# Reordering the weighing and scoring of head pairs in a two-layer graph attention kernel

## The chip, the cores and the metric

The kernel runs on one core of a Trainium2 chip. The metric is the device time of one execution in microseconds (us), as the median of several runs. The engines are called as in the profile: PE is TensorE (matmuls), PEld its weight loads, DVE is VectorE, ACT is ScalarE, POOL is GpSimd, and SP is SyncE, which only issues DMAs here. ACTq and SPq are DMAs issued from the queues of ScalarE and SyncE.

## The reference

64 graphs of 256 nodes with 512 features pass through two attention layers. Each layer normalises, applies a ReLU, attends over the graph's edges and adds the result to its input:

```python
# layer 0: 4 heads of 64, no bias on q, k, v
h = jnp.maximum(_layernorm(x, axis=-1), 0.0)
q, k, v = split_heads(h @ Wq), split_heads(h @ Wk), split_heads(h @ Wv)
sim = jnp.einsum('bhid,bhjd->bhij', q, k) * 64 ** -0.5
attn = jax.nn.softmax(jnp.where(adj[:, None], sim, -jnp.finfo(sim.dtype).max), axis=-1)
out = jnp.einsum('bhij,bhjd->bhid', attn, v)            # heads joined again
x = x + out @ Wo + bo
# layer 1: 8 heads of 64; a second layernorm with gamma and beta after the ReLU,
# the mask is adj | eye, masked scores are -1e9
h = jnp.maximum(_layernorm(x, axis=-1), 0.0)
...
x = x + out @ w_out.T + b_out
```

All matrices are float32.

## The kernel before

**Steps and periods.** `fast_path` takes two graphs in a step, so there are 32 steps `s`. (`general_path` is there for inputs with extreme scores and is entered only when a flag says so.) Work of several steps overlaps: in one *period* the kernel finishes layer 1 of step `s`, finishes layer 0 of step `s+1` and starts layer 0 of step `s+2`. In the profile a period lasts about 96.8 us; one visit at AT_X starts at 1553.24 us and the next at 1650.0.

**The order written by hand.** Instructions of PE, DVE, ACT and POOL are issued in the order in which the program makes them. That order is a list: `at(period, place, fn, ...)` (L1126) notes a piece of work with a number, and at the end (L1366) all pieces are sorted by it and run. Pieces with the same number keep the order in which they were noted. A place is about one product set of 12 us per unit, but between pieces that are close together only the order counts: 0.00002 after something means "right behind it on every engine that both use". DMAs of SyncE are issued by the same functions.

**Dense products.** Projections and output products are done in seven block products instead of eight (`project_qk` L805, `project_v0_turned` L855, `project_v1` L890, `combine` L905), each into a PSUM bank, with sums of blocks taken by ACT, DVE and POOL (`evacuate` L746, `accumulate` L765, `act_sums0` and `act_sums1` L404 to L410). The fourth product of a set adds into the bank of the first, so the first must have been copied out by ACT (L751, L759 or L770) before. [...] four go round as `ps_sc` ("sc" in the profile), four as `ps_mm` ("mm").

**Visits.** Between the dense sets stand visits (`visit`, L1143), three to a period: at AT_X before `project_v1`, at AT_Q0 before layer 0's projections, and at AT_Z before layer 1's first. A visit at place `w` takes heads in pairs `pr`. It *weighs* the two pairs of a previous unit, that is, it multiplies the exponentials with the values (`weigh`, L1034, matmuls at L1041, form 128\*32), and copies the result out on ACT (`weigh_out`, L1056). It *scores* the two pairs of a new unit (`scores`, L957, matmuls at L970, form 64\*128), adds the mask on DVE (`mask_scores`, L993, four instructions for each pair), and takes exponentials on ACT (`exponentials`, L998, four for each pair). Below, W0 and W1 are the weighings of the two pairs, S0 and S1 the scorings. W0 uses one sc bank, W1 one mm bank; S0 uses four sc banks; S1 uses two mm banks for the first graph and two sc banks for the second. In the kernel before, PE does W0, S0, W1, S1. Later, POOL adds halves of the keys (`key_halves`, L1005), DVE transposes and sums them (`turn_keys` L1011, `key_quarters` L1018, then L1071 to L1083), and POOL scales the weighed values by the inverse sums (`normalise`, L1116).

**Work beside a visit that the change touches.**

- `turn_values` (L874, DVE, one transpose at L878) turns layer 0's values, made by `project_v0_turned`, into a tile `values` that uses the same memory (tag "turned") as layer 1's `h`. It stands in the visit at AT_Z, behind the masks of S0.
- `place_h` (L714, ACT at L725 for layer 1) places the transposed `h` in `hT`, in four pieces `c`. Pieces 0 and 1 stand before the visit at AT_Z, at AT_H1; pieces 2 and 3 behind W0's copy.
- `scale_row` (L604, ACT at L606) scales one of the four row tiles of `h`. All four stand in the visit at AT_Q0 between W0's copy and the exponentials of S0. `turn_blocks` (L695, DVE at L700) reads them later.
- `load_graph` (L498, DMA from ACT's queue at L502) loads a step's `x` again, one graph at a time, into a buffer that `store_graph` (L947) empties. Both loads stand at AT_X behind W1's copy; POOL's `first_bias` (L508) reads them.

Of the kernel before, what the change touches and what calls it, by code (L numbers as in the profile page):

```python
# [315 lines left out]
def fast_path(  # L316
# [24 lines left out]
    NSTEP = B // G  # L341
# [62 lines left out]
    def act_sums0(b, eng=nc.gpsimd):  # L404
        eng.tensor_tensor(b[:, 3], b[:, 5], b[:, 0], ALU.subtract)
# [8 lines left out]
    HC, HP0, HP1 = NC // 2, PR0 // 2, PR1 // 2  # L414
# [711 lines left out]
    def at(period, place, fn, *args):  # L1126
        events.append((period * (PERIOD if period >= 0 else FIRST) + place, len(events), fn, args))

    def at_dense(period, place, length, fn, *args):

        rest = []
        at(period, place, lambda: rest.append(fn(*args)))
        at(period, place + length - LAST, lambda: rest[0]())

    def at_set(period, place, order, fn, *args):
        for i, n in enumerate(order):
            at_dense(period, place + i / 7, 1 / 7, fn, *args, n)
# [5 lines left out]
    def visit(period, w, prev, cur):  # L1143

        w -= 0.0003
        s, lyr, prs = prev
        last = (s, lyr) == (NSTEP - 1, 1)
        if prs:
            if prs[0] == 0 and not last:
                at(period, w - 0.0002, place_values, s, lyr)  # L1150
            if (s, lyr) == (1, 0):
                turned = sums = 0, 0.88
            elif 0 <= period < NSTEP - 2:
                sums = turned = (
                    (period, AT_X + 1.45) if abs(w - AT_Q0) < 0.01 else
                    (period, AT_V0 + 0.5595) if abs(w - AT_Z) < 0.01 else (period - 1, AT_Z + 1.25)
                )
                if abs(w - AT_Z) < 0.01:
                    turned = period, AT_V0 + 0.41
            else:  # L1160
                turned = sums = period, w - 0.0001
            at(*turned, turn_sums, s, lyr, prs)
            at(*sums, key_sums, s, lyr, prs)
            at(period, w - 0.00008, inverse_in, s, lyr, prs)
            for i, pr in enumerate(prs):
                if not last:
                    at(period, w + 0.0002 * i, weigh_out, s, lyr, pr, i == 1)
                    at(period, w + (0.55 if len(prs) == 1 else (0.3, 0.75)[i]), normalise, s, lyr, pr)
        z, q = w > AT_Z - 0.01 and period < NSTEP - 2, abs(w - AT_Q0) < 0.01 and 0 <= period < NSTEP - 2
        for i, pr in enumerate(cur[2]):  # L1170
            unit = (*cur[:2], pr)
            one = cur[:2] == (0, 0)
            at(period, w + 0.0002 * i, scores, *unit, i == 1)
            at(period, w + 0.0002 * i, mask_scores, *unit, 0)
            at(period, w + 1 / 7 if one else w + 0.0002 * i, mask_scores, *unit, 1)
            both = len(cur[2]) == 2
            for g, place in enumerate((0.05, 0.22) if one else ((0.00015, 0.00016) if both else (0.02, 0.03), (0.15, 0.3))[i]):
                at(period, w + place, exponentials, *unit, g)
            for e, place in enumerate((0.23, 0.3) if one else ((0.1, 0.11), (0.495, 0.496) if z else (0.435, 0.436) if q else (0.35, 0.36))[i]):
                if unit == (1, 0, 1):  # L1180
                    at(0, 0.45 + place, key_halves, *unit, e)
                else:
                    at(period, w + place, key_halves, *unit, e)
            if cur[:2] == (1, 0):
                period, w, key = 0, 0.0, (*cur[:2], (0, 1), pr)
                turn, add = ((0.44, 0.441), (0.715, 0.87))[pr]
            else:
                turn, add = (
                    ((0.31, 0.311), (0.6583, 0.6585))[pr] if one else ((0.49, 0.491), (0.63, 0.92))[i] if z else
                    ((0.43, 0.431), (1.02, 1.021))[i] if q else ((0.29, 0.291), (0.715, 1.001 if w < AT_X else 0.87))[i]  # L1190
                )
                key = (*cur, i)
            at(period, w + turn, turn_keys, cur[0])
            at(period, w + add, key_quarters, *key)

    AT_X, AT_C0, AT_QK, AT_Q0, AT_V0, AT_H1, AT_Z = 2.0, 3.0, 3.5, 4.5, 5.5, 6.06, 6.2
    LAST_QK = 4.0
    none, L0, L1A, L1B = (NSTEP, 0, ()), (0, 1), (0, 2), (1, 3)
    for s in range(NSTEP - 1):
        visit(s, AT_X, (s + 1, 0, L0), (s, 1, L1A))  # L1200
        if s < NSTEP - 2:
            visit(s, AT_Q0, (s, 1, L1A), (s, 1, L1B))
            visit(s, AT_Z, (s, 1, L1B), (s + 2, 0, L0))

    p = NSTEP - 2
# [15 lines left out]
    for s in range(NSTEP):  # L1221

        p = s - 2
# [41 lines left out]
        if s < 2:  # L1265
            for t in range(NT):
                place = (FIRST_V0 + 0.14 * t - (0 if t else 0.0005), (4.31, 5.02, 5.16, 5.31)[t])[s]
                at_dense(p, place, 0.14, project_v0, s, t)
        else:
            for i, n in enumerate(SET):  # L1270
                at_dense(p, AT_V0 + 0.08 * i, 0.08, project_v0_turned, s, n)
            at(p, AT_Z - 0.0002, turn_values, s)
            at(p, 6.6, move_values, s, 0)
            at(p, 6.98, move_values, s, 1)
        p = s - 1
        if s == 0:
            p -= 2.23 / FIRST
        edge = 0 if s == 0 else 1 if s == NSTEP - 1 else 2
        if edge < 2:
            at(p, (0.0, 0.2)[edge], load_x, s)  # L1280
        else:
            at(p, AT_X + 0.005 if s > 1 else 1.2, load_graph, s, 1)
            at(p, AT_X + 0.0051 if s > 1 else 1.2, load_graph, s, 0)
        for k, t in enumerate(NORM1):
            at(p, (1.55, 1.5, (2.34, 2.5, 2.85, 2.86)[k])[edge], first_bias, s, t)
# [10 lines left out]
        for k in range(NT):  # L1296
            at(p, ((2.901, 3.041, 3.181, 3.321), (2.99919, 2.99933, 2.99947, 2.99961), (3.79, 3.8, 3.94, 3.95))[edge][k], norm1, s, k)
            at(
                p, ((3.042, 3.182, 3.322, 3.323), (2.99948, 3.2, 3.3, 3.45), (4.08, 4.22, 4.23, 4.37))[edge][k],
                norm1_rest, s, k,  # L1300
            )
            at(*((0, 3.6 + 0.001 * k), (p, 6.5 + 0.1 * k), (p, 5.6 + 0.01 * k))[edge], second_bias, s, k)
            place = ((3.6112, 3.6113, 3.7502, 3.7503)[k], 3.6 + 0.01 * k, AT_Q0 - 0.0002 + 0.00001 * k)[edge]
            at(p, place, scale_row, s, NORM1[k])
            if edge == 2:
                at(p, AT_Q0 + (0.15, 0.16, 0.29, 0.3)[k], turn_blocks, s, 1, NORM1[k])
# [2 lines left out]

        turn = (3.763, 3.9995, AT_H1)[edge]  # L1310
        for c in range(NC):
            at(
                p, turn + 0.00001 * c if edge < 2 or c < HC else AT_Z - 0.00029 + 0.00001 * c,
                transpose_h if edge < 2 else place_h, s, 1, c,
            )
        at(p, turn + (0.001, 0.0001, 0.155)[edge], lambda s=s: act_sums0(S[s]["hT"]))
        at(p, turn + (0.002, 0.0001, 0.156)[edge], lambda s=s: act_sums1(S[s]["hT"]))
        p = s
        if s < NSTEP - 1:
            at_set(p, 0.0, SET, project_qk, s, 1, 0)  # L1320
            at_set(p, 2.0, SET, project_v1, s)
            at_set(p, AT_QK if s < NSTEP - 2 else 3.0, SET, project_qk, s, 1, 1)
            p, place = (s + 1, 1.0) if s < NSTEP - 2 else (s, LAST_QK + 2)
            at(p, place - 0.24, lambda s=s: act_sums0(S[s]["oT1"]))
            at(p, place - 0.23, lambda s=s: act_sums1(S[s]["oT1"]))
            at_set(p, place, SETC, combine, s, 1)
            at(p, place + 6 / 7 + 0.001, store_graph, s, 1)
            at(p, place + (0.99975 if s < NSTEP - 2 else 0.9994), store_graph, s, 0)
        else:
            p = s - 1  # L1330
            at_set(p, LAST_QK, SET, project_qk, s, 1, 0)
            at_set(p, LAST_QK + 1, SET, project_qk, s, 1, 1)
            at_set(p, LAST_QK + 3, SET, project_v1, s)
            at(p, LAST_QK + 4.015, lambda s=s: act_sums0(S[s]["oT1"], nc.vector))
            at(p, LAST_QK + 4.035, lambda s=s: act_sums1(S[s]["oT1"], nc.vector))
            at_set(p, LAST_QK + 4.1, SETC, combine, s, 1)
            for n, (i, j) in enumerate(((0, 0), (0, 1), (1, 1), (1, 0))):
                at(p, LAST_QK + 4.1 + (3, 6, 5, 7)[n] / 7, store_block, s, i, j)
# [14 lines left out]
    for i in range(16):  # L1353

        place = (
            *(3.3 - 3.93 + (1 + k) / 7 - 0.0005 for k in range(7)), 0.5205,
            *(0.53 + 0.14 * (k + 1) - 0.0005 for k in range(4)), *(FIRST + (2 + k) / 7 - 0.0005 for k in range(4)),
        )[i]
# [61 lines left out]
```

## Time and profile before

| | us |
|---|---|
| median of 3 runs | 3144.71 |
| lowest and highest | 3144.18, 3145.71 |
| the profiled execution | 3143.63 |
| its span, first to last instruction | 3141.5 |
| granted TensorE clock | 1.0 of full speed |

The span is shorter than the time of the same execution by 2.1 us, which lie before the first and after the last instruction. The costliest groups on the engines that a visit uses, from part 5 of the profile's page (busy us, mean ns of one):

| line and engine | what | count | busy us | mean ns |
|---|---|---|---|---|
| L970 PE | scoring, sc banks | 2320 | 296.5 | 386 |
| L1041 PE | weighing, sc banks | 3152 | 190.8 | 382 |
| L993 DVE | mask, sc banks | 579 | 361.6 | 678 |
| L998 ACT | exponentials | 766 | 433.0 | 624 |
| L606 ACT | scale_row | 252 | 184.9 | 805 |
| L1005 POOL | key_halves | 383 | 479.3 | 1274 |

Matmuls are pipelined: one is listed with 380 ns although the next starts 216 ns after it. So times between starts say more than durations or busy time.

### The profile page before, as it was taken

The numbers are of one execution on the slowest core, as the hardware profiler recorded it, in microseconds if no ns is written. First come the engines' busy times: TensorE is split into PE (matmuls) and PEld (weight loads), VectorE is DVE, ScalarE is ACT, GpSimd is POOL, SyncE is SP. The second block draws the span as 40 slices with busy tenths as digits, with TensorE's granted clock in tenths as the row PEclk, the third lists the DMA queues.
The fourth block names the chain that finished last, engine by engine and source line by source line (L and its number), as shares of the span: only waits on it lengthen the run. The fifth ranks groups of instructions, "written<-read, shape, count | busy, mean of one in ns | idle before, by whom it ended". The sixth has DMA issues, their size and how long they took to land.

```text
span 3141.5 us, 55627 instructions
## 1 busy us (share of the span) xinstructions
PE 3125.5 (99%) x20362; PEld 2524.9 (80%) x20362; DVE 2462.6 (78%) x4371; ACT 1218.3 (39%) x2166; POOL 2244.6 (71%) x2128
## 2 busy tenths in 40 slices
PE   9999999999999999999999999999999999999999
PEld 7887888887888878788787888888787878878777
DVE  6877877878877778777787777877777877778766
ACT  4434343334334343433434333343434343343431
POOL 7877776776767767767777677776776766777753
PEclk9999999999999999999999999999999999999999
DMA  4233132232222332223313233222232222331211
GB/s 140 62 96 92 52 93 72 89 92 72 78 74 81 92 91 60 83 72 98 92 52 92 71 91 92 67 82 72 85 92 85 67 82 72 99 91 52 90 34 49
DMA packets 187590, 251.23 MB, mean 80 GB/s; under 512 B 58088, under 2 KB 78192, under 8 KB 187312
## 3 DMA queue, kind: packets, MB, share of 16 engines
q1 hardware_dynamic: 139088, 183.74, 20.3%
q10 hardware_dynamic: 48224, 63.87, 6.8%
q8 instruction: 164, 2.69, 0.4%
q14 instruction: 114, 0.93, 0.1%
HBM read 128.59 MB, written 34.34 MB: 52 GB/s over the span
## 4 chain that ended last, share of the span: by engine, by line
PE 98%; DVE 1%; POOL 1%; DMA 0%; ACT 0%; issue 0%; SPq 0%; ACTq 0%; DVEq 0%; POOLq 0%
PE mm L817 37%; PE mm L914 18%; PE mm L898 12%; PE sc L970 9%; PE mm L864 6%; PE sc L1041 6%; PE mm L1041 5%; PE mm L970 3%; PE mm L847 1%; PE mm L563 0%; PE mm L940 0%; PE mm L466 0%; PE mm L675 0%; POOL pd L1005 0%; POOL wqk L652 0%
## 5 line engine op out<-in xcount | busy, mean ns | idle before, releaser
L817 PE MATMUL mm<-hT,wqkv 128*128 128x256 f32 x3584 | 788.3, 380 | 0.0
L817 PEld LDWEIGHTS mm<-hT,wqkv 128*128 128x128 f32 x3584 | 677.6, 190 | 102.6 <-issue 11.7
L1005 POOL TENSOR_TENSOR pd<-p 128x512 f32<-128x512 f32 x383 | 479.3, 1274 | 307.8 <-DVE turned_p L1011 181.8
L914 PE MATMUL mm<-wo,oT 128*128 128x256 f32 x2632 | 585.5, 380 | 0.5
L914 PEld LDWEIGHTS mm<-wo,oT 128*128 128x128 f32 x2632 | 497.4, 190 | 78.7 <-issue 11.5
L998 ACT ACTIVATE p<-p 128x512 f32<-128x512 f32 x766 | 433.0, 624 | 95.8 <-DVE p L993 95.8
L993 DVE TENSOR_TENSOR p<-sc,n 128x512 f32<-128x512 f32 x579 | 361.6, 678 | 60.1 <-PE sc L970 60.1
L898 PE MATMUL mm<-wqkv,hT 128*128 128x256 f32 x1792 | 402.1, 382 | 0.4 <-ACT v L751 0.4
L817 PE MATMUL mm<-hT,wqk 128*128 128x256 f32 x1792 | 398.7, 382 | 0.0
L817 PEld LDWEIGHTS mm<-hT,wqk 128*128 128x128 f32 x1792 | 338.3, 191 | 55.7 <-issue 10.3
L898 PEld LDWEIGHTS mm<-wqkv,hT 128*128 128x128 f32 x1792 | 335.5, 190 | 54.2 <-issue 10.3
L970 PE MATMUL sc<-qk 64*128 64x256 f32 x2320 | 296.5, 386 | 1.4 <-DVE p L993 1.4
L785 POOL TENSOR_TENSOR xt<-xt,u 128x512 f32<-128x512 f32 x183 | 231.5, 1272 | 85.9 <-DVE xt L774 37.1
L970 PEld LDWEIGHTS sc<-qk 64*128 64x128 f32 x2320 | 221.3, 186 | 61.7 <-issue 39.5
L1011 DVE STREAM_TRANSPOSE turned_p<-pd 128x1024 f32<-128x1024 f32 x192 | 237.0, 1234 | 27.3 <-POOL pd L1005 27.3
L606 ACT ACTIVATE h<-h,mr,r 128x512 f32<-128x512 f32 x252 | 184.9, 805 | 171.7 <-POOL mr L602 171.7
L1116 POOL TENSOR_TENSOR oT<-oT 128x512 f32<-128x512 f32 x188 | 240.1, 1277 | 2.6 <-DMA oT<-line 2.6
L1018 DVE TENSOR_REDUCE part<-turned_p 128x32 f32<-128x1024 f32 x192 | 233.1, 1214 | 4.4
L508 POOL TENSOR_TENSOR xt<-xt,bo_b 128x512 f32<-128x512 f32 x124 | 156.3, 1273 | 56.2 <-DMA xt<-in_x_dram 50.9
L1041 PE MATMUL sc<-p,v 128*32 128x256 f32 x3152 | 190.8, 382 | 0.0
L864 PE MATMUL mm<-hT,wv 128*128 128x256 f32 x840 | 188.6, 382 | 0.0
L993 DVE TENSOR_TENSOR p<-mm,n 128x512 f32<-128x512 f32 x187 | 120.4, 686 | 85.9 <-PE mm L970 85.9
(153 smaller groups left out, 4282.1 us busy)
## 6 DMA issues: line engine op xcount, KB each, us to landing
h<-blocks SPq DMA_DIRECT2D x960, 64.0 KB, 2.0
oT<-line SPq DMA_DIRECT2D x376, 128.0 KB, 3.0
h<-in_x_dram SPq DMA_DIRECT2D x31, 1024.0 KB, 7.7
xt<-in_x_dram ACTq DMA_DIRECT2D x60, 512.0 KB, 5.3
out_dram<-xt SPq DMA_DIRECT2D x31, 512.0 KB, 3.1
out_dram<-xt ACTq DMA_DIRECT2D x31, 512.0 KB, 4.3
v<-values ACTq DMA_DIRECT2D x480, 32.0 KB, 1.9
ne<-ne SPq DMA_DIRECT2D x90, 64.0 KB, 2.0
```

Of the source, the lines that this page charges most:

```text
L817: nc.tensor.matmul(bank[:, k, :], w[:, wa, c, k, a * P:(a + 1) * P], st["hT"][:, ba, c, :], start=first and (k, c) == (0, 0), stop=(k, c) ...
L864: nc.tensor.matmul(bank, wv0[:, wa, c, :], st["hT"][:, ba, c, :], start=first and c == 0, stop=c == HC - 1, skip_group_check=True,)
L898: nc.tensor.matmul(bank[:, t, :], st["hT"][:, ba, c, t * P:(t + 1) * P], wqkv1[:, wa, c, 2, :], start=first and (t, c) == (0, 0), stop=(t, ...
L914: nc.tensor.matmul(bank[:, t, :], oT[:, ba, c, t * P:(t + 1) * P], w[:, wa, c, :], start=first and (t, c) == (0, 0), stop=(t, c) == (NIC - ...
L970: nc.tensor.matmul(sc[g][e][:, kc, :], qk[rows, 1, k0:k0 + P], qk[rows, 0, g * N:(g + 1) * N], start=True, stop=True,)
L993: nc.vector.tensor_tensor(p[e][:, g], sc[e], neg[:, :, g, :], ALU.add)
L998: nc.scalar.activation(p[e][:, g], p[e][:, g], AF.Exp, scale=SCALE)
L1005: nc.gpsimd.tensor_tensor(st["pd"][:, e], p[e][:, :, 0, :], p[e][:, :, 1, :], ALU.add)
L1011: nc.vector.transpose(st["turned_p"], st.pop("pd").rearrange("p e g (b k) -> p (e g b) k", k=32))
L1018: nc.vector.tensor_reduce(st["part", lyr, prs][:, i], st.pop("turned_p"), axis=mybir.AxisListType.X, op=ALU.add)
L1041: nc.tensor.matmul(po[r0:r0 + 32, g, :], (st["v1"][:, g * NIC + kc, pr * P + r0:pr * P + r0 + Q] if lyr else st["v0"][:, r0 // Q, pr, g * ...
L1116: nc.gpsimd.tensor_tensor(dst, dst, invb, ALU.mult)
```

## The change

It moves work in the hand-written order; no instruction is added or taken away. Both weighings now stand ahead of both scorings: W0, W1, S0, S1. `turn_values` moves ahead of the visit at AT_Z, to 6.13, and the last two pieces of `place_h` join the first two at AT_H1. Of the four `scale_row` at AT_Q0 two stay and two go behind S0's exponentials. Of the two loads at AT_X the first moves between S0's exponentials of the first and the second graph; the other keeps its place behind S0's exponentials, with W1's copy now ahead of them. `store_graph` of the first graph, from ACT's queue, stands behind W0's copy as before, and now ahead of W1's.

```diff
             for i, pr in enumerate(prs):
                 if not last:
-                    at(period, w + 0.0002 * i, weigh_out, s, lyr, pr, i == 1)
+                    at(period, w + 0.00002 * i, weigh_out, s, lyr, pr, i == 1)
...
-            at(period, w + 0.0002 * i, scores, *unit, i == 1)
-            at(period, w + 0.0002 * i, mask_scores, *unit, 0)
-            at(period, w + 1 / 7 if one else w + 0.0002 * i, mask_scores, *unit, 1)
+            at(period, w + 0.00003, scores, *unit, i == 1)
+            at(period, w + 0.00003, mask_scores, *unit, 0)
+            at(period, w + 1 / 7 if one else w + 0.00003, mask_scores, *unit, 1)
...
-            at(p, AT_Z - 0.0002, turn_values, s)
+            at(p, 6.13, turn_values, s)
...
-            at(p, AT_X + 0.005 if s > 1 else 1.2, load_graph, s, 1)
+            at(p, AT_X - 0.000145 if s > 1 else 1.2, load_graph, s, 1)
             at(p, AT_X + 0.0051 if s > 1 else 1.2, load_graph, s, 0)
...
-            place = ((3.6112, 3.6113, 3.7502, 3.7503)[k], 3.6 + 0.01 * k, AT_Q0 - 0.0002 + 0.00001 * k)[edge]
+            place = ((3.6112, 3.6113, 3.7502, 3.7503)[k], 3.6 + 0.01 * k, AT_Q0 + (-0.0002, -0.00019, 0.0002, 0.00021)[k])[edge]
             at(p, place, scale_row, s, NORM1[k])
...
         for c in range(NC):
-            at(
-                p, turn + 0.00001 * c if edge < 2 or c < HC else AT_Z - 0.00029 + 0.00001 * c,
-                transpose_h if edge < 2 else place_h, s, 1, c,
-            )
+            at(p, turn + 0.00001 * c, transpose_h if edge < 2 else place_h, s, 1, c)
...
-            at(p, place + (0.99975 if s < NSTEP - 2 else 0.9994), store_graph, s, 0)
+            at(p, place + (0.99971 if s < NSTEP - 2 else 0.9994), store_graph, s, 0)
```

In `visit`, `w` is the place less 0.0003, and the exponentials of S0 stand at `w + 0.00015` and `w + 0.00016`.

## The prediction

> **What bounds the kernel now.** I read the page first, its busy shares and its chain of waits:
>
> ```profile
> PE 3125.5 (99%) x20362; PEld 2524.9 (80%) x20362; DVE 2462.6 (78%) x4371; ACT 1218.3 (39%) x2166; POOL 2244.6 (71%) x2128
> PE 98%; DVE 1%; POOL 1%; DMA 0%; ACT 0%; issue 0%; SPq 0%; ACTq 0%; DVEq 0%; POOLq 0%
> ```
>
> TensorE is the chain, nearly without a break. Then the waits of TensorE alone (us in total, times, longest):
>
> ```profile
> PE mm L734 <- ACT h L632: 7.0, 3, 6.5
> PE sc L970 <- DVE p L993: 1.4, 2, 0.9
> PE mm L847 <- DVE qk L761: 0.4, 1, 0.4
> PE mm L898 <- ACT v L751: 0.4, 1, 0.4
> ```
>
> They sum to 9.2 us of 3141.5: no wait is worth removing. What is left is the spacing of the matmuls. The timeline of TensorE through one visit (at AT_Z, before a step's layer-1 projections) has starts and lengths:
>
> ```profile
> 1521.28 1.93 PE L1041 MATMUL sc<-p,v 128*32 128x256 f32 x32
> 1523.14 2.00 PE L970 MATMUL sc<-qk 64*128 64x256 f32 x16
> 1525.07 1.93 PE L1041 MATMUL mm<-p,v 128*32 128x256 f32 x32
> 1526.93 1.13 PE L970 MATMUL mm<-qk 64*128 64x256 f32 x8
> 1527.90 1.03 PE L970 MATMUL sc<-qk 64*128 64x256 f32 x8
> 1528.86 3.50 PE L817 MATMUL mm<-hT,wqkv 128*128 128x256 f32 x15
> ```
>
> Take starts, since the ends are modelled. Weighing (L1041) lasts 1.864 us until scoring starts, scoring (L970) 1.928 us until the next form starts, 7.584 for the visit; the 93 visits of this kind repeat it within 2 ns, but for two exceptions below. Inside a block the starts of successive groups are 0.216 us apart. At a change of form (128\*32, 64\*128, 128\*128) I find 0.31 to 0.33 instead, and 0.24 (into 128\*32) or 0.32 (into the other two) for the group after. So a change costs 0.12 to 0.22 us, and a visit has five.
>
> What a block costs without a change shows in the tail: four weighings in a row, from the chain of waits,
>
> ```profile
> 3115.80 7.04 PE sc L1041 x128
> ```
>
> and a visit that does not weigh, two scorings in a row, in the timeline of TensorE:
>
> ```profile
> 3085.21 2.00 PE L970 MATMUL sc<-qk 64*128 64x256 f32 x16
> 3087.04 1.03 PE L970 MATMUL mm<-qk 64*128 64x256 f32 x8
> 3089.01 1.73 PE L970 MATMUL sc<-qk 64*128 64x256 f32 x8 [0.94 <-DVE p L993]
> ```
>
> The second scoring starts 1.83 after the first, not 1.93. Its second half then waits for VectorE: it writes the two score banks that the first scoring filled first, and the masks must have been read out of them. In single instructions, its weight load starts 0.053 us after the first mask ends (3088.958 to 3089.011). The change makes this wait regular.
>
> One more wait is hidden in the busy time. At AT_Q0 the first scoring takes 2.01, in the chain of waits, not 1.93:
>
> ```profile
> 1593.91 2.01 PE sc L970 x16
> ```
>
> Its last bank was W0's, whose copy (L1056) ends only at 1594.748, behind four place_h. The weight load starts at 1594.799, 0.193 later than due, and its matmul is 461 ns instead of 376: 0.085 lost. So the first 0.108 of such a lateness is free.
>
> **What the Trainium skill says.** TensorEngine Tiling (Array Packing), Key Properties: changing the tiling mode drains TensorE, changing the tile does not. The trace agrees: 0.31 instead of 0.216 at each change. Perfetto Trace Analysis, Identifying the Most-Contended Engine: matmul busy share is no measure of the distance to the roofline. It agrees: the drains hide in the 99%. TensorE: Matmul & The Clock Gate, Step-by-step: what each phase is for: weight loads are pulled ahead of running matmuls. It agrees: a load starts a group (0.21 us) ahead of its matmul, so a bank must be free that much earlier. PSUM — Partial Sum Buffer, Engine vs sequencer instructions: ScalarE and VectorE are strict FIFO. The trace shows it in the copy behind place_h, and so every moved instruction delays all behind it.
>
> **The change, part by part**, in us from a visit's first weighing matmul.
>
> *Weigh both, score both.* Two changes of form go. Weighing saves (4 x 1.864 - 7.045) / 3 = 0.137 per join. Joined scorings are 1.831 apart, which carries an entry of 0.104 (0.320 - 0.216); a further one takes 1.727, less 0.003 for its closer pairs, so 1.928 - 1.724 = 0.204 is saved. Together 0.341. New starts: W0 0, W1 1.75, S0 3.59, S1 5.42, projection 7.24. Visits with two pairs on both sides: 31 + 30 + 30 in the loop and 2 at the end. In the first (at 99.9 us; its last scoring takes 3.20) VectorE comes late with statistics and sets the end: it saves nothing. 92 x 0.341 = 31.4 us. W0's bank is then needed by a weight load at 4.35, and W0's copy ends at 2.77 at AT_Q0: the 0.085 goes too, 30 times, 2.6 us.
>
> *The wait that comes closer.* Score banks go round in a ring of four: W0 takes a; S0 b, c, d, a; S1's second half b, c. That half starts at 5.42 + 0.86 = 6.28, its weight loads at 6.07. VectorE starts S0's first mask 1.17 after S0 and ends the second 2.45 after it, at 6.04; with 0.053 of hand-over c is free at 6.10, 0.02 to 0.03 late. By the 0.108 above this is free, which I take. From above: the prefetch is lost, a first matmul taking 480 ns instead of 376, plus the lateness: 0.13 per visit, 12 us. A gain is excluded, as a wait only adds.
>
> *turn_values to 6.13, place_h's last two to AT_H1* (30 visits at AT_Z). turn_values now stands before the masks and waits for the fourth place_h. The four start at 0.16, 0.72 apart, the last takes 0.80: until 3.1. turn_values lasts 1.23: until 4.5. The first mask can start at 4.76. Cover 0.26 plus the free 0.08; without it the masks slip, and the late bank with them. W0's copy, now behind all four, ends at about 3.7, before 4.35. The masks are no longer split by turn_values.
>
> *scale_row halved* (30 visits at AT_Q0). ScalarE had copy, four scalings, exponentials, copy. Now both copies (the second at 3.73 to 4.31), two scalings until 5.8, exponentials until 8.0, two scalings until 9.4. The next product's copy (L751) is due at 9.3. TensorE does not wait: the product that reuses its bank is the fourth, at 7.24 + 0.10 + 3 x 1.73 = 12.5.
>
> *Loads of xt* (29 visits at AT_X). ScalarE before, in a visit that began at 1553.24:
>
> ```profile
> 1557.10 2.36 ACT L998 ACTIVATE p<-p 128x512 f32<-128x512 f32 x4 [1.28 <-DVE p L993]
> 1559.36 0.57 ACT L1056 COPY oT<-mm 128x512 f32<-128x512 f32 x1
> 1559.79 1.24 ACTq L502 DMA_DIRECT2D xt<-in_x_dram  x2
> 1562.85 0.59 ACT L751 COPY v<-mm 128x512 f32<-128x512 f32 x1 [2.92 <-PE mm L898]
> ```
>
> The first load waited until a store landed (1559.715). It now stands between the exponentials, reached at about 6.7 (1559.9), hardly later; then two exponentials until 8.0 and the other load, issued at about 8.0 to 8.5 (was 7.4). L751 is due at 9.3: covered. GpSimd's first_bias may get its rows 0.2 to 1 later; key_halves behind it wait for exponentials that end near 12 anyway. SP's queue keeps its order, but a DMA that shares a semaphore with an earlier one waits for that one's landing, and these pairings can shift: 0, or the third rival. store_graph 0 moves ahead of the second copy alone: nothing.
>
> *VectorE and GpSimd after.* The eight masks run to 9.63 (was 9.30) while the projection starts 0.34 earlier. Then come 1.29 (turn_blocks, AT_Q0) or 1.23 (L530, AT_Z), to 10.9; the second product is ready for its sum at about 11.1: nothing. GpSimd's sum of hT for that product ends at 1527.35; it starts at 1530.3.
>
> Sum: 31.4 + 2.6 - 0 = 34.0 us. The profiled execution took 3143.63 (span 3141.5 and 2.1 around it), giving 3109.6; the median of the runs stands 1.1 above it: **3110.7**.
>
> **Rivals.**
> - *The late bank costs its full 0.13 in each visit:* 34.0 - 12 = 22 saved, 3122.7. For: the two stalls of this kind took a 480 ns matmul. Against: those waits were 0.6 us and more, and AT_Q0 shows a late load partly free. Chance 0.09.
> - *VectorE loses its cover in one kind of visit* (place_h slower, turn_values behind it): masks 0.4 to 0.6 late, 30 times 0.3 to 0.5, 9 to 15 lost, about 3122. For: the cover is thin. Against: visits repeat within some 10 ns. Chance 0.08.
> - *Slower: ScalarE is stuck behind the second load at AT_X.* If its partner is the first load (5.3 us median to landing, 7.6 at most), it holds L751 and so the bank of the fourth product. With 6.8 + 7.6 = 14.4, L751 would end near 15.4, 2.9 after 12.5: 29 x 2.9 - 34.0 = 50 lost, 3195. It decides from 34.0 / 29 = 1.17 us per visit, L751 ending after 13.7. Against: the second load was let go by an earlier transfer until now (landed at 1560.62), and at the median landing the stall is 0.4. Chance 0.06.
> - *TensorE's order stays as it is:* 3144.7. Against: the timeline alternates, and the new places sort otherwise. Chance 0.02.
>
> **How the numbers follow.** The forecast has 0.75, 3109.7 to 3115 (up to 0.05 per visit for the late bank). The range's upper end, 3121, takes in about half of the first two rivals. What a measurement here tells from no change is 0.2%, 6.3 us. Faster 0.91 (the forecast and the first two rivals, less 0.01), same 0.03, slower 0.06.
>
> **What would show it.** Right: L1041 x64 and L970 x32 in one piece on TensorE, 7.24 to 7.26 us from first weighing to projection in all three kinds of visit, turn_values ending before 4.76, L751 at AT_X ending before 12.5. Wrong: a visit over 7.35, joined blocks spaced wider than 0.22, or waits of L898 or L817 for ScalarE.

## The result and the profile after

| | before | after |
|---|---|---|
| median, us | 3144.58 | 3115.64 |
| lowest to highest of 6 runs each | 3144.18 to 3145.71 | 3113.48 to 3116.32 |
| the profiled execution and its span | 3143.63, 3141.5 | 3115.69, 3113.6 |

The time is 0.9907 of that before (95% interval 0.9894 to 0.9919): 28.9 us less, where 34.0 were forecast. The median lies 4.9 above the forecast of 3110.7, just above the range that was given 0.75 (3109.7 to 3115) and inside the wider one (up to 3121). First the page of the kernel after, its busy shares and its chain:

```profile
PE 3091.8 (99%) x20362; PEld 2538.7 (82%) x20362; DVE 2453.8 (79%) x4371; ACT 1235.3 (40%) x2166; POOL 2242.3 (72%) x2128
...
PE 94%; POOL 3%; DMA 1%; DVE 1%; issue 1%; SPq 0%; ACT 0%; ACTq 0%; POOLq 0%; DVEq 0%
```

TensorE is called busy for 99% in both kernels, though one is 28 us shorter with the same 20362 matmuls: what went was counted as busy. POOL has 3% of the chain where it had 1%. The visit at AT_Z that began at 1507.76, in the timeline of TensorE of the kernel after (start, length):

```profile
1507.76 1.93 PE L1041 MATMUL sc<-p,v 128*32 128x256 f32 x32
1509.51 1.91 PE L1041 MATMUL mm<-p,v 128*32 128x256 f32 x32
1511.35 2.00 PE L970 MATMUL sc<-qk 64*128 64x256 f32 x16
1513.18 1.03 PE L970 MATMUL mm<-qk 64*128 64x256 f32 x8
1514.05 1.03 PE L970 MATMUL sc<-qk 64*128 64x256 f32 x8
1515.01 2.21 PE L817 MATMUL mm<-hT,wqkv 128*128 128x256 f32 x9
```

Both weighings in one piece, both scorings in one piece, and 7.25 us from first start to projection instead of 7.58. Then the waits of TensorE in the kernel after (us in total, times, longest):

```profile
PE mm L734 <- ACT h L632: 7.7, 3, 6.5
PE mm L914 <- DVE xt L774: 2.4, 5, 0.7
PE sc L970 <- DVE p L993: 1.7, 2, 0.9
PE mm L914 <- POOL oT L408: 1.5, 2, 0.8
PE mm L817 <- DVE qk L757: 0.6, 1, 0.6
PE mm L898 <- ACT v L751: 0.4, 1, 0.4
PE mm L847 <- DVE qk L761: 0.3, 1, 0.3
PE mm L817 <- ACT qk L751: 0.2, 1, 0.2
```

They sum to 14.8 us against 9.2 before. The growth is 5.6, and most of it stands in two lines that were not there: L914, `combine` of layer 0, 3.9 us. Laying the starts of the visits side by side in the two traces gives the whole account (us, sums over the run):

| stretch of TensorE | before | after | difference |
|---|---|---|---|
| all visits, first weighing to what follows | 712.9 | 679.2 | -33.7 |
| from AT_X visits to AT_Q0 visits (29) | 903.94 | 908.24 | +4.30 |
| from AT_Q0 visits to AT_Z visits (30) | 552.24 | 552.23 | 0.0 |
| from AT_Z visits to AT_X visits (30) | 731.30 | 731.97 | +0.67 |
| start to the first visit | 39.69 | 40.37 | +0.7 |
| the rest and the end | | | +0.2 |
| sum: the spans | 3141.5 | 3113.6 | -27.9 |

The counts of 29 and 30 leave out steps at the two ends, which are built otherwise and stand in the row of the rest. So the visits gave what was forecast, and some 4 us were lost in the stretch behind AT_X, in `combine`. The start scatters from 39.0 to 40.7 over the kernels profiled here, whatever their edits.

**What `combine` waits for.** One of the six late stretches, in the visit at AT_X that began at 2880.53. From the timelines of ScalarE, POOL and TensorE of the kernel after, in order of start:

```profile
2882.73 0.43 ACTq L948 DMA_DIRECT2D out_dram<-xt  x1
...
2886.07 1.23 ACT L998 ACTIVATE p<-p 128x512 f32<-128x512 f32 x2 [1.23 <-DVE p L993]
2889.63 0.38 ACTq L502 DMA_DIRECT2D xt<-in_x_dram  x1
2890.06 0.63 ACT L998 ACTIVATE p<-p 128x512 f32<-128x512 f32 x1 [2.76 <-DVE p L993]
...
2890.76 2.51 POOL L1005 TENSOR_TENSOR pd<-p 128x512 f32<-128x512 f32 x2 [8.07 <-ACT p L998]
...
2901.42 0.73 POOL L408 TENSOR_TENSOR oT<-oT 128x256 f32<-128x256 f32 x1
...
2902.20 4.58 PE L914 MATMUL mm<-wo,oT 128*128 128x256 f32 x20 [0.71 <-POOL oT L408]
2907.44 1.10 PE L914 MATMUL mm<-wo,oT 128*128 128x256 f32 x4 [0.65 <-DVE xt L774]
```

And the view of the line of `store_graph` in that window, its landing:

```profile
L948 ACTq DMA_DIRECT2D out_dram<-xt x1: 427/427/427, 2882.7 to 2882.7; - x1
...
DMA to landing us min/median/max: 6.8/6.8/6.8
```

The store issued at 2882.73 lands 6.8 us later, at 2889.5, and only then does the load go, at 2889.63, 9.10 into the visit. The exponentials of S0's second graph stand behind it, and the bracket of 2890.06 shows 2.76 us of idle time (it names the mask, but the masks of S0 had ended at 2887.8; what it waited for stands a line higher). `key_halves` of the first pair reads both graphs of a head, so it waits for the third exponential, and starts at 10.23 (2890.76 - 2880.53). In the kernel before it started at 5.71 in nearly every step. POOL's work keeps the order of the list, so its sums of oT (L408) end at 21.62, and TensorE stops twice. Over the 29 steps the sums end at 19.51 at the earliest. In the six steps where they end at 20.09 or later `combine` stops, and in no other (19.88 at most); these stops sum to 3.9 us. In the kernel before they ended at 19.85, but the combine also came 0.34 later, with the longer visit.

Not all six have this cause. In five of them `key_halves` starts at 8.70 or later, POOL then works without a break, and L408 ends 11.4 us on: the held exponentials set the end, for 2.5 us of stops. In the sixth, the visit that began at 2304.75, the load went at 6.40 and `key_halves` started at 7.53, but the load took 7.4 us to land where 4.3 were usual. POOL waited for its rows, and 1.4 us of stops followed:

```profile
2318.75 1.27 POOL L508 TENSOR_TENSOR xt<-xt,bo_b 128x512 f32<-128x512 f32 x1 [2.74 <-DMA xt<-in_x_dram]
...
2326.48 4.58 PE L914 MATMUL mm<-wo,oT 128*128 128x256 f32 x20 [0.77 <-POOL oT L408]
```

### The profile page after: what moved, and what is told of

Read it like the earlier page. It is cut to its first block, busy times and chain, and to the rows that moved or that the text cites. A ratio compares the mean times of both kernels' runs of the same rounds, so it can differ in the third digit from the quotient of the medians.

```text
span 3113.6 us, 55568 instructions
## 1 busy us (share of the span) xinstructions
PE 3091.8 (99%) x20362; PEld 2538.7 (82%) x20362; DVE 2453.8 (79%) x4371; ACT 1235.3 (40%) x2166; POOL 2242.3 (72%) x2128
## 4 chain that ended last, share of the span: by engine, by line
PE 94%; POOL 3%; DMA 1%; DVE 1%; issue 1%; SPq 0%; ACT 0%; ACTq 0%; POOLq 0%; DVEq 0%
PE mm L817 37%; PE mm L914 17%; PE mm L898 11%; PE sc L970 8%; PE mm L864 6%; PE sc L1041 6%; PE mm L1041 5%; PE mm L970 2%; POOL pd L1005 1%; POOL xt L508 1%; PE mm L847 1%; DMA h<-blocks 0%; PE mm L940 0%; DMA out_dram<-xt 0%; PE mm L563 0%
## 5 line engine op out<-in xcount | busy, mean ns | idle before, releaser
L817 PE MATMUL mm<-hT,wqkv 128*128 128x256 f32 x3584 | 788.3, 380 | 0.6 <-DVE qk L757 0.6
L817 PEld LDWEIGHTS mm<-hT,wqkv 128*128 128x128 f32 x3584 | 677.6, 190 | 103.2 <-issue 11.4
L914 PE MATMUL mm<-wo,oT 128*128 128x256 f32 x2632 | 586.1, 380 | 4.2 <-DVE xt L774 2.4
L914 PEld LDWEIGHTS mm<-wo,oT 128*128 128x128 f32 x2632 | 497.3, 190 | 83.2 <-issue 9.2
L998 ACT ACTIVATE p<-p 128x512 f32<-128x512 f32 x766 | 440.8, 626 | 118.2 <-DVE p L993 106.2
L817 PE MATMUL mm<-hT,wqk 128*128 128x256 f32 x1792 | 398.7, 382 | 0.3 <-ACT qk L751 0.2
L817 PEld LDWEIGHTS mm<-hT,wqk 128*128 128x128 f32 x1792 | 338.3, 191 | 55.9 <-issue 10.3
L970 PE MATMUL sc<-qk 64*128 64x256 f32 x2320 | 294.0, 385 | 1.7 <-DVE p L993 1.7
L970 PEld LDWEIGHTS sc<-qk 64*128 64x128 f32 x2320 | 218.1, 186 | 62.8 <-issue 27.9
L864 PEld LDWEIGHTS mm<-hT,wv 128*128 128x128 f32 x840 | 156.5, 190 | 27.2 <-ACT vT L751 6.2
L1041 PE MATMUL mm<-p,v 128*32 128x256 f32 x2976 | 177.6, 379 | 0.0
```

The lines of the kernel that those rows point to most:

```text
L817: nc.tensor.matmul(bank[:, k, :], w[:, wa, c, k, a * P:(a + 1) * P], st["hT"][:, ba, c, :], start=first and (k, c) == (0, 0), stop=(k, c) ...
L864: nc.tensor.matmul(bank, wv0[:, wa, c, :], st["hT"][:, ba, c, :], start=first and c == 0, stop=c == HC - 1, skip_group_check=True,)
L914: nc.tensor.matmul(bank[:, t, :], oT[:, ba, c, t * P:(t + 1) * P], w[:, wa, c, :], start=first and (t, c) == (0, 0), stop=(t, c) == (NIC - ...
L970: nc.tensor.matmul(sc[g][e][:, kc, :], qk[rows, 1, k0:k0 + P], qk[rows, 0, g * N:(g + 1) * N], start=True, stop=True,)
L998: nc.scalar.activation(p[e][:, g], p[e][:, g], AF.Exp, scale=SCALE)
L1041: nc.tensor.matmul(po[r0:r0 + 32, g, :], (st["v1"][:, g * NIC + kc, pr * P + r0:pr * P + r0 + Q] if lyr else st["v0"][:, r0 // Q, pr, g * ...
```

## The experiments

The theory after the comparison: the shorter visits are real and free of new waits (the late bank costs nothing), and the loss lies in the first load standing between the exponentials, with a store's landing in front of it. Rivals: the loss comes from the load being later or slower itself; the gain needs only the new order of TensorE, and the other moves are beside the point; the halved `scale_row` has a part in it.

### e1_order_only: TensorE's order alone, on the kernel before

```diff
-                    at(period, w + 0.0002 * i, weigh_out, s, lyr, pr, i == 1)
+                    at(period, w + 0.00002 * i, weigh_out, s, lyr, pr, i == 1)
...
-            at(period, w + 0.0002 * i, scores, *unit, i == 1)
+            at(period, w + 0.00003, scores, *unit, i == 1)
```

with the masks' places, as in the change; `turn_values`, `place_h`, `scale_row`, the loads and the store stay.

> The kernel before with the two weighings ahead of the two scorings, and none of the other moves. Theory (the gain is the two changes of form per visit; what is lost again comes from the load of xt at AT_X): every visit of the three kinds takes 7.245 us from first weighing to projection as in the changed kernel, because nothing of the other moves stands ahead of what TensorE waits for; but the first load at AT_X is issued near 8.0 us of the visit instead of 6.4 to 7, so GpSimd's first_bias and layer 0's sums of oT come later and the output product (L914) waits 0.1 to 1 us in most steps: 3116 to 3128 us. Rival (the other moves are the cover without which the visits stall): visits of 7.4 us or more at AT_Z or AT_Q0, with waits of L970 for VectorE or ScalarE, and 3125 us or more with no wait of L914.

Measured: 3170.14 us (3170.05 to 3173.72), 1.0086 of before (1.0069 to 1.0102). Slower by 25 us, which neither theory had: the first was right about the visits and about L914, which stops in 17 of 29 steps, but the larger loss, at AT_Z, was in neither. The visits are 7.245 us in all three places, so the gain of 33.7 is there, but behind each visit at AT_Z 1.70 us are lost (26.07 instead of 24.37 to the next visit, 30 times, 51 us), and 10 between AT_X and AT_Q0. From the timelines of VectorE, POOL and TensorE of this kernel, behind the visit that began at 1532.70:

```profile
1542.25 1.24 DVE L878 STREAM_TRANSPOSE values<-vT 128x1024 f32<-128x1024 f32 x1
...
1543.63 2.49 POOL L1005 TENSOR_TENSOR pd<-p 128x512 f32<-128x512 f32 x2 [1.31 <-DVE values L878]
...
1546.16 1.25 DVE L1011 STREAM_TRANSPOSE turned_p<-pd 128x1024 f32<-128x1024 f32 x1 [0.82 <-POOL pd L1005]
...
1548.58 0.68 DVE L755 TENSOR_TENSOR qk<-mm,qk 128x512 f32<-128x512 f32 x1
...
1549.31 1.99 PE L817 MATMUL mm<-hT,wqkv 128*128 128x256 f32 x8 [0.46 <-DVE qk L755]
...
1551.25 0.65 DVE L757 TENSOR_TENSOR qk<-mm,qk 128x512 f32<-128x512 f32 x1
...
1552.04 1.97 PE L817 MATMUL mm<-hT,wqkv 128*128 128x256 f32 x8 [0.74 <-DVE qk L757]
```

Reading downward: `turn_values` (L878), noted behind S0's masks, now comes behind all eight masks, since S1's masks have moved up. POOL's `key_halves` starts when it ends: its result pd and vT have one buffer by turns (tag "pd"), which vT gives up only when turned. The next line on VectorE, `turn_keys`, waits 0.82 for POOL, and the product sums queued behind it (L755, L757) let TensorE wait twice (1.20 us by the brackets, 1.70 by the starts, since ends are modelled). The view of L878's line shows that this is the rule:

```profile
who waited for it (us, times):
  POOL pd L1005: 38.1, 30
```

In the kernel before nobody waited for it. The other 10 us: the store stands behind W1's copy here and lands at 7.3 to 8.8 us of the visit, the load goes only then, POOL waits for its rows, and the oT sums end at 20.0 or later in most steps.

### e2_moves_only: the other moves alone

The kernel after with TensorE's order and the masks as in the kernel before (the diff of e1 backward).

> The changed kernel with the old order on TensorE: W0, S0, W1, S1; all the other moves stay. Theory: visits take 7.58 us again, 7.67 at AT_Q0 where W0's copy is still behind place_h, and no time is gained: 3143 to 3149 us, the upper part if the load that holds the exponentials makes GpSimd late as it does in the changed kernel. Rival (the moves are worth something by themselves, as they free ScalarE and VectorE): under 3140 us.

Measured: 3173.32 us (3171.05 to 3174.14), 1.0090 (1.0073 to 1.0107): slower by 29, and again not what was expected. The visits account for 27 of it, and the stretch behind AT_X for 2.4. At AT_X and AT_Q0 the visits are as before, 7.58 and 7.67; at AT_Z they take 8.46, 0.88 more, 30 times. From the timelines of ScalarE and TensorE of this kernel:

```profile
1537.32 1.93 PE L1041 MATMUL sc<-p,v 128*32 128x256 f32 x32
...
1537.47 2.93 ACT L725 ACTIVATE hT<-h,gb 128x512 f32<-128x512 f32 x4 [2.27 <-PE mm L864]
...
1539.18 1.56 PE L970 MATMUL sc<-qk 64*128 64x256 f32 x10
...
1540.31 0.56 ACT L1056 COPY oT<-sc 128x512 f32<-128x512 f32 x1
...
1540.93 1.13 PE L970 MATMUL sc<-qk 64*128 64x256 f32 x6 [0.19 <-ACT oT L1056]
1541.98 1.93 PE L1041 MATMUL mm<-p,v 128*32 128x256 f32 x32
```

All four `place_h` (L725) now stand ahead of W0's copy, which ends at 3.55 us of the visit; S0, right behind W0, needs W0's bank for its last quarter, by the single instructions from 2.83 on. TensorE stops in the middle of S0, which takes 2.80 us from start to start instead of 1.93. The bracket shows only 0.19: the modelled ends hide the rest. This is the lateness that cost 0.085 at AT_Q0 in the kernel before, made 0.8 us larger. With W1 in between, as in the change, the bank is needed at 4.35.

So each half of the change costs 25 to 29 us alone, and both together gain 29. They are one change.

### e7_turn_back: which of the moves the order needs

The kernel after with `turn_values` and the last two `place_h` at their old places:

```diff
-            at(p, 6.13, turn_values, s)
+            at(p, AT_Z - 0.0002, turn_values, s)
```

and the old lines of `place_h`.

> The changed kernel with turn_values and the last two place_h back in the visit at AT_Z, where turn_values now comes behind all eight masks. Theory (the tile that turn_values reads shares its memory with the tile that key_halves write; late, it makes GpSimd, then turn_keys, then the sums that free banks late): visits stay at 7.245 us, key_halves at AT_Z start right after turn_values, near 10.9 us, and the stretch between the visits at AT_Z and AT_X takes 26.1 us instead of 24.4, with waits of L817 for VectorE: 3163 to 3168 us. Rival (what cost time in the run with the new order alone was the scalings or the loads): 3115 to 3120 us.

Measured: 3163.51 us (3162.18 and 3164.84), 1.006 (1.004 to 1.008). From AT_Z to AT_X 26.07, as in e1, 50.2 us more than in the kernel after; the waits of TensorE hold

```profile
PE mm L817 <- DVE qk L757: 22.1, 30, 0.7
PE mm L817 <- DVE qk L755: 13.7, 30, 0.5
```

The same two waits, 30 times each. The place of `turn_values` (with `place_h`, which must go ahead of it) accounts for e1's loss behind AT_Z. That the shared buffer of vT and pd is the link is read from the chain above; giving vT memory of its own was not tried.

### e6_four_changes: is the gain the number of changes of form?

The kernel after with W1 last: W0, S0, S1, W1, four changes of form in place of three (and five before).

```diff
-                    at(period, w + 0.00002 * i, weigh_out, s, lyr, pr, i == 1)
+                    at(period, w + 0.0002 * i, weigh_out, s, lyr, pr, i == 1)
```

> The changed kernel with the second weighing behind both scorings: W0, S0, S1, W1, four changes of form in a visit instead of three (changed kernel) or five (before). Theory (a visit costs its matmuls at 0.216 us a group plus 0.12 to 0.22 us for each change of form): visits at AT_X take 7.38 us, at AT_Q0 7.38 to 7.47 since W0's copy is late again. At AT_Z the masks stand behind turn_values, which ends near 4.5 us, so S1's second half waits and the visit takes 8.2 us or more. Rival (the gain came from W1 being earlier, not from the number of changes): 7.58 us at AT_X, as before.

Measured: 3165.8 us in a single run, for the visits' lengths only. The timeline of TensorE at AT_X:

```profile
1469.86 1.93 PE L1041 MATMUL sc<-p,v 128*32 128x256 f32 x32
1471.72 2.00 PE L970 MATMUL sc<-qk 64*128 64x256 f32 x16
1473.56 1.03 PE L970 MATMUL mm<-qk 64*128 64x256 f32 x8
1474.42 1.03 PE L970 MATMUL sc<-qk 64*128 64x256 f32 x8
1475.38 1.93 PE L1041 MATMUL mm<-p,v 128*32 128x256 f32 x32
1477.24 3.07 PE L898 MATMUL mm<-wqkv,hT 128*128 128x256 f32 x13
```

7.383 us in 30 of the 31 visits at AT_X, 7.467 in 30 of 31 at AT_Q0; the first visit, in which VectorE comes late, takes 13.37. So five changes make 7.583, four 7.383, three 7.245: joining the scorings is worth 0.200, joining the weighings 0.138, where the prediction had 0.204 and 0.137. The rival falls: W1 is last here, and 0.200 are gained all the same. At AT_Z it is 8.518, mainly for e2's reason: W0's copy ends late behind `place_h`, and 30 waits of L970 for it are in the view. That cost 0.88 in e2; the other 0.26 are a second stop in S1, behind late masks, which is the one that had been expected.

### e3_load_back, e4_xt_reuse, e5_xt_early: what the load costs

Three kernels around the first load. e3 puts it back behind all four exponentials:

```diff
-            at(p, AT_X - 0.000145 if s > 1 else 1.2, load_graph, s, 1)
+            at(p, AT_X + 0.005 if s > 1 else 1.2, load_graph, s, 1)
```

> The changed kernel with the first load of xt back behind all four exponentials of S0. Theory A (in the changed kernel it costs time that the load holds two exponentials until a store lands): key_halves of the first pair start at 7.4 us of the visit in every step, L914 waits nearly never, 3111 to 3113 us. Theory B (the load's landing matters more than the hold): it is issued near 8.0 us and lands 1.3 us or more later than in the changed kernel, first_bias and the second pair's key_halves behind it slip, L914 waits in most steps, 3117 to 3128 us.

Measured: 3114.08 us (3113.50 to 3117.18), 0.9907 (0.9890 to 0.9923). `key_halves` starts at 7.38 in nearly every step, but the load goes only at 7.36 to 8.5, lands at 11.2 to 12.8, and the oT sums still end as late as 20.7; in every step POOL now waits for the load's rows. Waits of L914: 1.6 us in place of 3.9; by starts, the stretch from AT_X to AT_Q0 takes 905.9 us in place of 908.2. One lateness is exchanged for another, the time lies between the ranges of the two theories, and the run times overlap with those of the kernel after: not told apart by time, only by the waits.

e4 leaves the load's place and takes away what it waits for. The load of each step asks for a fresh tile xt, which takes the memory of an old one, and the first load waits for the stores of both graphs of the old tile, of which ScalarE's lands last. Where the tile itself is used again, each load waits only for the store of its own half:

```diff
-            S[s]["xt"] = io.tile([P, NT, D], FP, name="xt")
+            S[s]["xt"] = S[s - 2]["xt"] if s > 1 else io.tile([P, NT, D], FP, name="xt")
```

> The changed kernel, but a step from the third on uses the same tile for xt as the step two before, instead of a new tile in the same memory, so that the load of one graph's rows waits only for the store of the same rows (which landed 3.3 us after the visit's start) and not for the other graph's. Theory (the store of the other graph holds the load, which holds two exponentials, which make GpSimd's sums for L914 late): the load is issued by 6.5 us in every step, the waits of L914 shrink from about 3.9 us to under 1.5 us in all, 3111 to 3113.5 us. Rival (the waits of L914 come from the masks, which run 0.33 us later on VectorE): waits and time as in the changed kernel, 3115 to 3116 us.

Measured: 3112.07 us (3111.55 to 3113.11), 0.9898 (0.9881 to 0.9914), all runs below all runs of the kernel after. In 20 of 29 steps the load goes at 6.22, with no wait between the exponentials (6.49 to 7.46 in the others, where the theory had 6.5 at most); L914 waits 1.3 us, in two steps in which the load went at 6.22. In one of these it landed only at 13.15; in the other the second load went only at 11.17 and held the second pair's exponentials (why so late is open). The stretch takes 905.6 us.

e5 is e4 with the load moved ahead of the exponentials, right behind W1's copy. Without the reuse all four exponentials would stand behind both stores there; that was not tried.

```diff
-            at(p, AT_X - 0.000145 if s > 1 else 1.2, load_graph, s, 1)
+            at(p, AT_X - 0.00027 if s > 1 else 1.2, load_graph, s, 1)
```

> The reused xt tile, and the first load of xt moved up to stand right behind W1's copy, ahead of all exponentials. Theory: the load waits only for a store that has landed by 3.5 us, is issued by 4.4 us of the visit and lands near 8.5 us, so that first_bias never waits for it past 12 us and ScalarE is not held: the waits of L914 go to under 0.5 us in all, 3110 to 3112 us. Rival (an earlier load crowds the transfers of inverse sums and blocks that are in flight then, and these come late instead): POOL waits longer in normalise or the second load lands later, 3112 to 3116 us.

Measured: **3110.69 us (3110.44 to 3110.85), 0.9892 (0.9875 to 0.9908)**, the fastest version found, 5.0 us under the kernel after. The step shown above, in the timelines of ScalarE, POOL and TensorE of this kernel (the visit began at 2877.33):

```profile
2879.52 0.42 ACTq L948 DMA_DIRECT2D out_dram<-xt  x1
...
2881.12 0.39 ACTq L502 DMA_DIRECT2D xt<-in_x_dram  x1
2882.87 2.36 ACT L998 ACTIVATE p<-p 128x512 f32<-128x512 f32 x4 [1.23 <-DVE p L993]
...
2884.71 2.50 POOL L1005 TENSOR_TENSOR pd<-p 128x512 f32<-128x512 f32 x2 [5.22 <-ACT p L998]
...
2896.11 0.73 POOL L408 TENSOR_TENSOR oT<-oT 128x256 f32<-128x256 f32 x1
...
2897.27 6.46 PE L914 MATMUL mm<-wo,oT 128*128 128x256 f32 x28
```

The load goes at 3.79 and the four exponentials are one run; `key_halves` starts at 7.38 (10.23 in the kernel after), L408 ends at 19.51 (21.62), and `combine` is one piece. The load itself lands only at 11.50, 7.7 us after its issue, where the theory had 8.5: it goes 5.3 us earlier than in the kernel after and lands 1.7 earlier. Other transfers in flight, as the rival had it, may be what slows it; that isn't shown. It cost no time in this step; in one other, POOL waited for a late load and L914 for 0.4 us. ScalarE's store lands at 8.66, nearly as late as in the kernel after; only the second load waits for it now, with no exponential of S0 behind it. Over all steps L914 waits 0.5 us, and from AT_X to AT_Q0 it takes 904.33 us, 0.4 more than in the kernel before and 3.9 less than in the kernel after.

How much the load costs changes from kernel to kernel with the landings: e6 and e7 have it in the same place as the kernel after, between the exponentials, and lost only 1.0 and 1.2 us in this stretch. Each kernel has one profile, so this scatter isn't measured further; the six times of the kernel after spread over 2.8 us, the four of e5 over 0.4.

### e9_early_scale4: the halved scale_row

e5 with all four `scale_row` ahead of the exponentials, as before the change.

> As the run with the reused tile and the early load, with all four scale_row back ahead of the exponentials at AT_Q0. Theory (nothing of TensorE waits for these exponentials within a microsecond or two): visits at AT_Q0 and the stretch behind them stay as they are, the time within 0.5 us of the run without this edit. Rival (the exponentials, 1.5 us later, make key_halves and what hangs on them late): waits of L817 or L864 in the stretch from AT_Q0 to AT_Z, 0.1 to 0.5 us in each of 30 steps, 3 to 15 us more.

Measured: 3112.00 us (3110.70 to 3112.64), 0.9895 (0.9878 to 0.9911). Visits at AT_Q0 7.245 all the same, the stretch behind them 552.27 us against 551.93 in e5. The rival's 3 to 15 us are excluded. But the medians differ by 1.3 us, where the theory allowed 0.5, and three of the four runs lie above all of e5. Of the 1.8 us between the two profiled spans 0.3 lie in the stretch behind AT_Q0, the rest in the other stretches and at the start; that the halving has any part in them is not shown.

## Why the prediction was right, and where it was off

- *Weigh both, score both*: right. 33.7 us measured in the visits, 34.0 forecast with AT_Q0's 0.085, and e6 confirms each price of a join. The reading behind it was that a change of form costs time that the busy share hides; the Trainium skill, TensorEngine Tiling (Array Packing), Key Properties, says that a change of tiling mode drains TensorE, and 7.583, 7.383 and 7.245 us for five, four and three changes agree. The first visit saved nothing (8.858 before, 8.873 after), as said.
- *The wait that comes closer*: right as free. With 0.13 for each visit they would have been 7.37 long; they are 7.245 in all three places. In the visit shown the second mask ended 6.05 us in (forecast 6.04), and the weight load behind it started 0.02 late and cost nothing. That rival falls.
- *turn_values to 6.13, place_h*: right. In the visit shown VectorE's transpose ended 4.38 us in (forecast 4.5) and the first mask started 4.76 in, as forecast; over the 30 visits the transpose ends by 4.57 and the first mask never starts after 4.76. The rival in which VectorE loses its cover falls too. What the prediction did not see is that these moves aren't incidental: without `turn_values` ahead, TensorE's order loses 50 us (e1, e7), and without TensorE's order `place_h` ahead loses 27 (e2).
- *scale_row halved*: right as far as it was measured; with all four ahead the visits at AT_Q0 last the same (e9).
- *Loads of xt*: this is the term that was mis-sized, 0 where 3.9 us were lost: so much are the waits of L914 in the kernel after, and so much shorter is its stretch in e5. (The other 1.0 of e5's gain lies at the start and in other stretches.) Two errors stand in its lines. "Reached at about 6.7, hardly later" was read in one visit, whose store landed at 6.48; over the run they land at 5.88 to 9.00 in the kernel after, and the kernel before already showed 5.91 to 7.78. And of what stands behind the held load only first_bias and the second pair's `key_halves`, which wait until near 12 anyway, were counted, not the first pair's, which went from 5.71 to 7.4 at least. Nor was it counted that the visit's 0.34 comes off the time that POOL has for the oT sums. This hold made 2.5 of the 3.9 us. The other 1.4 are one load that landed late, 7.4 us after it was issued, though the prediction's own lines had up to 7.6 for a landing. e3 takes away the hold alone and makes the landing later, e5 takes away the hold and lets the load go earlier; only then is the loss gone.
- *VectorE and GpSimd after*: the sums of VectorE were in time but for one step (0.6 us for L757 in the waits above, which e3, e4, e5 and e9 show as well). Of the signs of being wrong that were named, one came that the kernel before did not have: L817 waited for ScalarE, once, for 0.2 us.
- The slower rival looked at the right place, a DMA holding ScalarE's queue at AT_X, but through the wrong work behind it: even in the worst step L751 ended 11.15 us into the visit, against the 12.5 at which it would be needed. Nor did the second load wait for the first one's landing: it was issued before it in all 29 steps. What was late was POOL, in six of 29 steps, through the exponentials in five of them.

The forecast was built on the profiled execution: a span 34.0 us shorter. The two spans differ by 27.9. Of the 6.1 us between, about 4 are the load; 0.7 lie at the start and 0.7 in the one stop behind AT_Z, which no experiment here tells from scatter, and 0.3 in the visits. (The medians are only 5.1 short, since the kernel before was profiled in an execution 0.95 us under its median.) That the time still fell inside the stated range is in part luck: the upper part of the range was drawn for two rivals that did not come, and the load, put at nothing, used some of it.

## What to carry to other kernels

Where an engine alternates between forms, price each change from starts, not from busy time, and give the reordering the moves that cover its new neighbours: here each half of the change, tried alone, cost time, and the whole gained. A DMA put between two instructions of a computing engine brings the landing that it waits for into that engine's queue; read the spread of such landings over all steps, not one, and follow everything behind it to the engine that needs it. If a load waits for a whole buffer's old stores, using the same tile again lets each part wait for its own store; here that gained 3.6 us, and 5.0 with an earlier place for the load, while putting the load back in the order gained nothing that the times tell.

## What was not expected of the hardware

- The price of a change of form can be read elsewhere and carried over. Four weighings and two scorings in a row, near the end of the kernel before, gave 0.137 and 0.204 us for a join; e6 and the kernel after show 0.138 and 0.200 in the middle of the loop.
- A stop in the middle of scoring costs more than the wait. In single instructions of e2, S0's matmuls start two by two, 0.216 us from pair to pair; when one half lacked its bank, the other half went on alone for two starts, and at the end the late half ran its last two alone, so that the 16 took ten starts instead of eight: 0.43 us, beside 0.35 of standing still and 0.10 for starting again.
- Stores of 512 KB from ScalarE's and SyncE's queues took 2.8 to 6.8 us to land in the kernel after (median 4.1), 2.8 to 5.6 in the kernel before, and one load of 512 KB 7.4 us (issued at 6.40 of its visit, landed at 13.78) where 4.3 were usual. The early load of e5 took 7.7 us in the one step where its landing is told: an earlier issue moved the landing by much less than itself.
